# A two-layer graph network on one core: the second layer's first feed-forward product by block products, layer norm's rows on ScalarE, new durations in the plan

## The chip, the core and the metric

The kernel runs on one core of one Trainium2 chip. The metric is the device time of one execution in microseconds (us). The core has five engines, each with a queue of its own: TensorE (PE, matrix products; its weight loads appear as PEld), VectorE (DVE), ScalarE (ACT, which evaluates functions from loadable tables), GpSimd (POOL) and SyncE (SP, which here issues all the DMA transfers). Products land in PSUM, of which there are 8 banks of 512 float32 columns on 128 partitions. All is float32.

## The reference, cut to what matters

64 graphs of 256 nodes with 256 features go through two layers; each layer ends in a feed-forward block of width 1024 between two layer norms.

```python
# layer 0: two graph-attention steps, then
h = _layernorm(residual + h, g_ln1, b_ln1)
ff = jnp.matmul(jax.nn.relu(jnp.matmul(h, w_ff1) + b_ff1), w_ff2) + b_ff2
x = _layernorm(h + ff, g_ln2, b_ln2)
# layer 1: 8-head attention with a mask for each of 4 relations, then
x = _ln(src + attn_out, g1, beta1)
ff = jax.nn.gelu(x @ W1 + b1, approximate=False) @ W2 + b2
return _ln(x + ff, g2, beta2)
```

Layer norm is (x - mean) * rsqrt(var + 1e-5) * g + b over the 256 features of a node.

## The kernel before, in words

**Pairs and ways.** The 64 graphs are worked on as 32 pairs, so that a matrix product can have 512 columns (two graphs of 256 nodes). `whole_way` (L896) is a generator that takes one pair through everything: `gat_layers` (the two graph attentions), `feed_forward` with stage 0 (Relu), `attention` (stage 1), `feed_forward` with stage 2 (Gelu), then the output's DMA. Each `yield` stands before a step on TensorE and names the events it has to wait for, an exclusive name ("gat", "ff", "attention": one pair at a time) and the PSUM banks and buffers it takes.

**A plan decides the order.** `run` simulates the engines while the kernel is built. Three pairs are under way at once. At each moment it lets the engine go on that is free earliest; TensorE gets the first ready step, by preference one of the pair that holds "ff". Work for the other engines is handed in by `put(engine, us, emit, *events, ...)` with a duration, a rank, buffers it needs or frees, and a lag after which its result counts as there. The emitted order of each engine is then fixed (`keep_order`). On the chip each engine takes its instructions in this order and waits on real semaphores, so wrong durations in the plan change the order of work, not what is computed. Buffers are rings: `free` lists their slots for the plan, the `bufs` argument of `tile` makes them.

**First feed-forward product.** The input comes transposed as yT (features on partitions; two chunks of 128). Without blocks (stage 2 before, L651 to L660) each of 8 tiles of 128 hidden features is two accumulated products of 128x128 weights with 512 columns, and one activation of 512 columns out of PSUM. With blocks (stage 0, L565 to L653) the 2x2 block scheme of Winograd's variant of Strassen's method is used: two halves of the features, two halves of the 1024 hidden features, two halves of the nodes; seven block products in place of eight. `first_weights` loads the weights in four pieces into a tile of seven slots, `block_sums` forms three of the missing slots and one more by four VectorE operations at the start (L834). For each pair `sum_of_blocks` (L557) makes four 128x256 differences on VectorE, partly in place in yT, in the tile `sums_yT` (one buffer). `Slabs` stands for two of the four tiles of a half: its steps p1 to p7 are two 256-wide products each (L586); `evacuate` (L592) copies intermediate sums from PSUM by ScalarE, `add` (L598) adds others by VectorE, `activate` (L573) applies the function to 256 columns. p6 waits for p1's evacuation, p7 for p6's, p4 for p7's. The two objects a and b go through the steps in turn, in the order of the list at L650. One record of a float32 product in the profile stands for half of it: each product shows two.

**Second product** (L671): 32 products of 256 columns, followed by `add_rows` (L451, VectorE) and layer norm.

**Layer norm** (L453 to L480) works on one graph of the pair, two row tiles of 128x256: `statistics` on VectorE (L463, L464); `root` on GpSimd adds epsilon and raises to the power -0.5 (L467, L468); meanwhile `centre` on VectorE forms (x - mean) * g (L472), and `scale` on VectorE multiplies by the root and adds b (L476). It runs four times per pair for each graph: after the graph attentions, after each feed-forward block and after attention.

**The transposition.** `transposed` (L487) turns 32x32 blocks on VectorE (L496), stores them in memory (L501, SP) and gathers them as yT by four transfers (L507, SP); yT has three buffers. For a few `hurried` pairs at the start and the end TensorE transposes instead (L527). Stage 0 and 2 hold yT until the first product is done; attention copies it to yTa at once (L707, ScalarE).

Of the kernel before, what the change touches and what calls it, by code (L numbers as in the profile page):

```python
# [10 lines left out]
F32 = mybir.dt.float32  # L11
# [16 lines left out]
SLACK = 0.5  # L28
BY_BLOCKS = (0,)
START = {"tensor": 12.0, "vector": 11.0, "scalar": 12.0, "gpsimd": 0.0, "sync": 40.0}  # L30
# [3 lines left out]
def two_layers(ctx: ExitStack, tc: tile.TileContext, t: dict, out: bass.AP, flag: bass.AP):  # L34
# [91 lines left out]
    def bank():  # L126
# [11 lines left out]
    alone = {}  # L138
    free = {name: [0.0] * n for name, n in (("bank", 8), ("a", 2 * HQ), ("m", 2 * HQ), ("h", 2 * HQ), ("yb", 2), ("yT", 3), ("yTa", 1),
                                             ("xT", 1), ("rows", 1), ("e", 2), ("adjT", 1), ("adj", 3), ("sums", 1), ("x", 4))}  # L140
# [13 lines left out]

    def put(engine, us, emit, *events, rank=1, lag=0.15, kb=0, function=None, needs=None, frees=(), event=None):

        piece = {"engine": engine, "us": us, "emit": emit, "rank": rank, "lag": lag, "kb": kb, "function": function,
                 "needs": needs, "frees": frees, "event": event or Event(), "ready": 0.0, "missing": 0}  # L160
        for e in events:
            if e.time is None:
                piece["missing"] += 1
                e.then.append(piece)
            else:
                piece["ready"] = max(piece["ready"], e.time)
        if not piece["missing"]:
            waiting[engine].append(piece)
        return piece["event"]
# [190 lines left out]
    def gat_weights(y, at, at_home, ratio, there, to, empty, b):  # L360
# [20 lines left out]

        there = put("vector", 0.9, lambda: weigh(0), *there, rank=0, needs="e")
        there = put("vector", 1.0, lambda: weigh(1), there, rank=0, frees=["rows"] * b)
        return of, put("scalar", 0.85, scale, there, rank=0)

    def gat_layers(pair, to, loads):
# [12 lines left out]
        def evacuated(to, k, wide, ps):  # L399
            return put("scalar", 0.33, lambda: nc.scalar.activation(to[:, k, :wide], ps[:, :wide], AF.Copy),  # L400
                       took(0.88), frees=["bank"])
# [46 lines left out]
    def add_rows(y, p, b, *events):  # L448

        rows = y[:, of_graph(b), :].rearrange("p k d -> p (k d)")  # L450
        return put("vector", 0.65, lambda: nc.vector.tensor_tensor(rows, p, rows, ALU.add), *events, frees=["bank"])  # L451

    def layernorm(r, gb, b, *events):  # L453
        g, beta, _ = gb
        st = mv = rstd = None
        rows = [r[:, 2 * b + j, :] for j in range(2)]

        def statistics():
            nonlocal st, mv, rstd
            st, mv = small.tile([P, 2, 6], F32, name="st"), small.tile([P, 2, 2], F32, name="mv")  # L460
            rstd = small.tile([P, 2], F32, name="rstd")
            for j in range(2):
                nc.vector.bn_stats(st[:, j, :], rows[j])  # L463
                nc.vector.bn_aggr(mv[:, j, :], st[:, j, :])  # L464

        def root():
            nc.gpsimd.tensor_scalar(rstd, mv[:, :, 1], EPS, None, ALU.add)  # L467
            nc.gpsimd.tensor_tensor(rstd, rstd, mhalf[:, :2], ALU.pow)  # L468

        def centre():  # L470
            for j in range(2):
                nc.vector.scalar_tensor_tensor(rows[j], rows[j], mv[:, j, 0:1], g, op0=ALU.subtract, op1=ALU.mult)  # L472

        def scale():
            for j in range(2):
                nc.vector.scalar_tensor_tensor(rows[j], rows[j], rstd[:, j:j + 1], beta, op0=ALU.mult, op1=ALU.add)  # L476

        there = put("vector", 1.18, statistics, *events)
        power = put("gpsimd", 1.3, root, there)
        return put("vector", 0.95, scale, power, put("vector", 0.95, centre, there))  # L480

# [4 lines left out]
    def transposed(y, ready, to, b, pair, stage):  # L486
# [16 lines left out]
        def gather():  # L503
            if b == 0:
                to["yT"] = work.tile([P, 2, 4, KC * 64], F32, name="yT", bufs=3)
            for q in range(4):
                nc.sync.dma_start(to["yT"][32 * q:32 * q + 32, b],  # L507
                                  home[:, 128 * q:128 * q + 128].rearrange("(a j) n -> j a n", a=4))

        there = put("vector", 0.65, turn, ready, needs="yb")  # L510
        there = put("sync", 0.4, store, there, lag=1.3, kb=256, frees=["yb"])
        to[b] = put("sync", 1.75, gather, there, *([to[0]] if b else []), lag=1.7, kb=64, needs=None if b else "yT")

    def transposed_on_tensor(y, to):

        for b in range(2):
            if b == 0:
                yield [to[b]], None, 1, "yT"
                to["yT"] = work.tile([P, 2, 4, KC * 64], F32, name="yT", bufs=3)
            else:  # L520
                yield [to[b]], None, 1
# [14 lines left out]
    def feed_forward(y, normal, w, func, relieved, gb, pair, stage):  # L536
# [24 lines left out]
        if by_blocks:  # L561
            summed = [put("vector", 0.42, lambda: sum_of_blocks(0), normal[0], normal[1], rank=0, needs="sums")]
            for n in range(1, 4):
                summed.append(put("vector", 0.42, lambda n=n: sum_of_blocks(n), summed[-1], rank=0))

# [10 lines left out]
        class Slabs:  # L576
# [13 lines left out]
            def evacuate(self, name, rows, at, event):  # L590
                def copy():
                    nc.scalar.activation(self.rows[rows][:, :, at], self.bank["x"], AF.Copy)  # L592
                self.there[name] = put("scalar", 0.62, copy, event, rank=-1)

            def add(self, name, rows, at, bank, *events, frees=()):
                def add():
                    to = self.rows[rows][:, :, at]
                    nc.vector.tensor_tensor(to, self.bank[bank], to, ALU.add)  # L598
                self.there[name] = put("vector", 0.68, add, *events, rank=-1, frees=frees)

            def activate(self, rows, right, event):
                for n in range(2):
                    m, at = self.t + n + rows * half, columns[right]
                    of = self.rows[rows][:, n, at]
                    evacuated[right][m] = activate(of, of, m, 0.36, event, rank=right - 1)

# [22 lines left out]
            def p4(self):  # L629
# [4 lines left out]
                for n in range(2):  # L634
                    m = self.t + n + half
                    evacuated[0][m] = activate(self.rows[1][:, n, columns[0]], self.bank["x"][:, n], m, 0.36, there,
                                               rank=-1, frees=["bank"] * n)
# [8 lines left out]
        if by_blocks:  # L646
            a, b = Slabs(0), Slabs(2)
            for step in (a.p1, b.p1, a.p2, a.p6, b.p6, a.p5, a.p7, b.p7, b.p5, b.p2, a.p4, b.p4, a.p3, b.p3):
                yield from step()
            f = [f[m] for m in (0, 1, 4, 5, 2, 3, 6, 7)]  # L650
        else:  # L651
            for m in range(NF):
# [5 lines left out]
                if m % 2 == 0:  # L658
                    slabs()
                evacuated[0][m] = evacuated[1][m] = activate(f[m], p1, m, 0.6, took(1.72), frees=["bank"])  # L660
        frees_at(clock["tensor"], ["yT"] + ["sums"] * by_blocks)
# [27 lines left out]
    def projected(to, c, yT, w, bias, scale):  # L689
        ps = bank()  # L690
        for d in range(KC):
            nc.tensor.matmul(ps, lhsT=w[:, d, c * P:(c + 1) * P], rhs=yT[:, :, d, :], start=d == 0, stop=d == KC - 1)  # L692
        return put("scalar", 0.6, lambda: nc.scalar.activation(
            to[:, c, :], ps, AF.Identity, bias=bias[:, c:c + 1], scale=scale), took(1.72), relieved[1], frees=["bank"])

    def attention(y, normal, pair, all_adj):
# [12 lines left out]

        there = put("scalar", 0.55, lambda: in_one_piece(0), normal[0], needs="yTa")  # L710
        yield [put("scalar", 0.55, lambda: in_one_piece(1), there, normal[1], frees=["yT"])], "attention", 1
        qT, kT = (work.tile([P, KC, 512], F32, name=n) for n in ("qT", "kT"))
# [5 lines left out]
        def scores(n):  # L718
# [19 lines left out]
            def halves(o):  # L738
                h[n][o] = work.tile([P, N], F32, name="h", bufs=2 * HQ)
                nc.vector.tensor_tensor(h[n][o], a[n][o][:, :N], a[n][o][:, N:], ALU.add)  # L740

            there = [put("scalar", 0.52, lambda o=o: weight(o), there, rank=0, function="exp", needs="a", frees=["bank"])
                     for o in range(HQ)]
            masked.append([put("vector", 0.61, lambda o=o: mask(o), there[o], rank=0, needs="m") for o in range(HQ)] +
                          [put("vector", 0.36, lambda o=o: halves(o), there[o], rank=0, needs="h") for o in range(HQ)])

        def products(n):
# [18 lines left out]
            there = put("vector", 1.68, lambda: nc.vector.reciprocal(s, po[:, N:]), there, rank=0)  # L766
            there = put("vector", 0.36, lambda: nc.vector.tensor_tensor(to, po[:, :N], s, ALU.mult), there, rank=0)
            put("vector", 0.45, check, there, frees=["bank"])
# [82 lines left out]
    ln.append(layernorm_weights("L1_gnn_g1", "L1_gnn_beta1", "L1_gnn_b2"))  # L851
    ff1 = (weights("L1_gnn_W1p"), column("L1_gnn_b1"), weights("L1_gnn_W2"))
    ln.append(layernorm_weights("L1_gnn_g2", "L1_gnn_beta2"))
# [33 lines left out]
    def reliefs():  # L887
# [6 lines left out]
        yield [landed["ff1"]], None, 1  # L894
        put("vector", 0.0, lambda: None, relieve(ff1[1], lambda c, m: ff1[0][:, c, m * P:(m + 1) * P], ln[2][2]), event=relieved[2])

# [457 lines left out]
```

## Time and profile before

| | |
|---|---|
| median of 3 runs | 3125.2 us (3124.86 to 3127.16) |
| the profiled execution, whole | 3130.63 us |
| its span, first to last instruction | 3128.9 us |
| mean granted TensorE clock | 0.994 |
| VectorE: mask L736, 512 of 128x512 | 350.8 us busy |
| VectorE: L472 and L476 together, 1024 of 128x256 | 438.2 us busy |
| VectorE: statistics L463 and L464 | 208.5 and 93.2 us busy |
| GpSimd: L467 and L468, 256 each | 75.3 and 196.3 us busy |
| TensorE: L657, 1024 records of 512 columns | 457.1 us busy |
| TensorE: L586, 1024 and 768 records of 256 columns | 243.5 and 187.0 us busy |

A row of the profile names line, engine, operation, the tile written and the tiles read, the shape and the count, then the total busy time and the mean of one in ns. The mean holds a latency that overlaps with the next instruction of the same engine, so that the distance from one start to the next in the timeline is shorter than the mean. In the tables by stages each engine's busy time stands beside its count of instructions.

### The profile page before, as it was taken

The page shows a single profiled execution, that of the slowest core. Times are in us where ns is not written, and L with a number is a line of the kernel's source. Part 1 is how long each engine was busy: PE and PEld are TensorE (multiplying, and loading weights), DVE is VectorE, ACT ScalarE, POOL GpSimd, SP SyncE. Part 2 cuts the span into 40 slices and gives each one's busy share as a digit, 9 for nine tenths or more (in the row PEclk, how much of TensorE's full clock was granted, in tenths as well). Part 3 has the DMA queues.
Part 4 walks back from the last instruction along what each step waited for, and adds up shares of the span by engine and source line. Part 5 has one row for each costly group of instructions (what it writes and reads, how often), then busy time and mean ns, then how long its engine had stood idle before and what let it go on. Part 6 is the DMA issues. An engine that isn't in the chain of part 4 may idle for free.

```text
span 3128.9 us, 47274 instructions
## 1 busy us (share of the span) xinstructions
PE 3098.1 (99%) x17598; PEld 2165.6 (69%) x17598; DVE 2310.9 (74%) x5593; ACT 1308.1 (42%) x2552; POOL 272.3 (9%) x518
## 2 busy tenths in 40 slices
PE   7999999999999999999999999999999999999998
PEld 6766775686577668756865776687568657766855
DVE  5787677777767777777777677767777876787664
ACT  3444444443444444444434444444444344444432
POOL 0000100010010001000100100010001001000100
PEclk8999999999999999999999999999999999999999
DMA  6112311330132123113211320231132113102200
GB/s 190 42 35 68 108 41 41 95 95 32 44 109 67 35 68 108 41 41 97 93 33 43 113 67 31 68 108 41 41 102 88 35 47 110 64 31 68 67 2 15
DMA packets 210173, 205.41 MB, mean 66 GB/s; under 512 B 22161, under 2 KB 169745, under 8 KB 209937
## 3 DMA queue, kind: packets, MB, share of 16 engines
q1 hardware_dynamic: 209936, 202.32, 20.7%
q8 instruction: 141, 2.31, 0.3%
q14 instruction: 96, 0.78, 0.1%
HBM read 137.51 MB, written 64.73 MB: 65 GB/s over the span
## 4 chain that ended last, share of the span: by engine, by line
PE 97%; DVE 1%; DMA 1%; issue 1%; ACT 0%; SPq 0%; POOL 0%; POOLq 0%; DVEq 0%
PE ps L671 28%; PE ps L657 14%; PE ps L586 12%; PE ps L692 7%; PE ps L754 7%; PE ps L684 7%; PE ps L725 4%; PE ps L425 4%; PE ps L776 4%; PE ps L438 4%; PE ps L409 3%; PE ps L757 2%; PE ps L866 0%; PE ps L527 0%; DMA w_L_gnn_w_ff1p<-in_L_gnn_w_ff1p 0%
## 5 line engine op out<-in xcount | busy, mean ns | idle before, releaser
L671 PE MATMUL ps<-w_L_gnn_W,ff 128*128 128x256 f32 x2048 | 459.4, 381 | 0.0
L671 PE MATMUL ps<-w_L_gnn_w_ff,ff 128*128 128x256 f32 x2048 | 457.4, 380 | 0.0
L657 PE MATMUL ps<-yT,w_L_gnn_W1p 128*128 128x512 f32 x1024 | 457.1, 594 | 0.0
L736 DVE TENSOR_TENSOR m<-a,adj 128x512 f32<-128x512 f32 x512 | 350.8, 685 | 140.7 <-ACT a L732 140.7
L671 PEld LDWEIGHTS ps<-w_L_gnn_W,ff 128*128 128x128 f32 x2048 | 386.5, 190 | 75.3 <-issue 23.3
L671 PEld LDWEIGHTS ps<-w_L_gnn_w_ff,ff 128*128 128x128 f32 x2048 | 387.1, 190 | 60.7 <-issue 9.1
L732 ACT ACTIVATE a<-ps 128x512 f32<-128x512 f32 x512 | 265.6, 602 | 284.4 <-issue 177.9
L657 PEld LDWEIGHTS ps<-yT,w_L_gnn_W1p 128*128 128x128 f32 x1024 | 192.7, 190 | 215.4 <-issue 201.5
L467 POOL TENSOR_SCALAR rstd<-mv 128x2 f32<-128x2 f32 x256 | 75.3, 294 | 2827.9 <-DVE mv L464 2702.6
L766 DVE RECIPROCAL s<-ps 128x256 f32<-128x256 f32 x128 | 224.5, 1754 | 113.6 <-PE ps L757 113.6
L451 DVE TENSOR_TENSOR x<-ps,x 128x512 f32<-128x512 f32 x256 | 173.4, 677 | 129.4 <-PE ps L671 118.2
L573 ACT ACTIVATE ff<-ps,c_L_gnn_b 128x512 f32<-128x512 f32 x256 | 170.0, 686 | 234.5 <-PE ps L657 233.8
L586 PE MATMUL ps<-yT,w_L_gnn_w_ff1p 128*128 128x256 f32 x1024 | 243.5, 379 | 0.0
L684 PE MATMUL ps<-wv,yTa 128*128 128x512 f32 x512 | 238.7, 599 | 0.0
L592 ACT ACTIVATE ff<-ps 128x512 f32<-128x512 f32 x192 | 114.3, 596 | 268.7 <-PE ps L586 268.3
L370 DVE SCALAR_TENSOR_TENSOR e<-rows,ratio 128x256 f32<-128x256 f32 x256 | 122.2, 477 | 135.4 <-DMA rows<-row 123.1
L586 PEld LDWEIGHTS ps<-yT,w_L_gnn_w_ff1p 128*128 128x128 f32 x1024 | 194.3, 190 | 30.7 <-issue 4.6
L740 DVE TENSOR_TENSOR h<-a 128x256 f32<-128x256 f32 x512 | 213.7, 417 | 0.0
L463 DVE BATCH_NORM_STATS2 st<-x 128x6 f32<-128x256 f32 x512 | 208.5, 407 | 3.2
L400 ACT ACTIVATE xw<-ps 128x260 f32<-128x260 f32 (+1 forms) x256 | 97.8, 387 | 245.3 <-PE ps L409 181.7
L468 POOL TENSOR_TENSOR rstd<-rstd,mhalf 128x2 f32<-128x2 f32 x256 | 196.3, 767 | 21.4
L586 PE MATMUL ps<-sums_yT,w_L_gnn_w_ff1p 128*128 128x256 f32 x768 | 187.0, 382 | 0.0
(111 smaller groups left out, 4264.1 us busy)
## 6 DMA issues: line engine op xcount, KB each, us to landing
home<-yb SPq DMA_DIRECT2D x182, 256.0 KB, 2.0
yT<-home SPq DMA_DIRECT2D x728, 64.0 KB, 2.0
rows<-row SPq DMA_DIRECT2D x60, 512.0 KB, 3.9
xT<-in_xT SPq DMA_DIRECT2D x32, 512.0 KB, 3.8
x<-in_x SPq DMA_DIRECT2D x32, 512.0 KB, 4.0
out<-x SPq DMA_DIRECT2D x32, 512.0 KB, 3.4
adjT<-in_adjT SPq DMA_DIRECT2D x31, 512.0 KB, 5.2
w_L_gnn_w_ff1p<-in_L_gnn_w_ff1p SPq DMA_DIRECT2D x4, 256.0 KB, 6.0
```

The costliest lines, as they stand in the source:

```text
L463: nc.vector.bn_stats(st[:, j, :], rows[j])
L468: nc.gpsimd.tensor_tensor(rstd, rstd, mhalf[:, :2], ALU.pow)
L586: nc.tensor.matmul(self.bank[to][:, n], lhsT=w1[:, of, (self.t + n) * P:(self.t + n + 1) * P], rhs=rhs(), start=first and n == 0, stop=Tru ...
L657: nc.tensor.matmul(p1, lhsT=w1[:, c, m * P:(m + 1) * P], rhs=rhs, start=c == 0, stop=c == KC - 1)
L671: nc.tensor.matmul(p2[:, j * D:(j + 1) * D], lhsT=f[m][:, (2 * j + b) * P:(2 * j + b + 1) * P], rhs=w2[:, m, :], start=m == 0, stop=m == N ...
L684: nc.tensor.matmul(ps, lhsT=yT[:, b, c, jc * P:(jc + 1) * P], rhs=wv[:, c].rearrange("p r m -> p (r m)"), start=c == 0, stop=c == KC - 1)
L692: nc.tensor.matmul(ps, lhsT=w[:, d, c * P:(c + 1) * P], rhs=yT[:, :, d, :], start=d == 0, stop=d == KC - 1)
L732: nc.scalar.activation(a[n][o], ps[o], AF.Exp)
L736: nc.vector.tensor_tensor(m[n][o], a[n][o], adj, ALU.mult)
L740: nc.vector.tensor_tensor(h[n][o], a[n][o][:, :N], a[n][o][:, N:], ALU.add)
L754: nc.tensor.matmul(po[o * DH:(o + 1) * DH, :N], lhsT=v[b][:, jc, at:at + DH], rhs=e[o][:, jc * N:(jc + 1) * N], start=r == jc == 0, stop=r ...
L766: there = put("vector", 1.68, lambda: nc.vector.reciprocal(s, po[:, N:]), there, rank=0)
```

## The change

The second feed-forward block's first product takes the way by seven blocks too (`BY_BLOCKS`), with its weights in seven slots; yT goes from three buffers to two. Layer norm's rows are normalised by ScalarE, as root * x - mean * root, and VectorE multiplies by g and adds b in two operations over both row tiles, with g and b broadcast; epsilon is added on VectorE, and GpSimd multiplies -mean by the root. In the blocks b.p5 stands ahead of a.p7 now. Durations and the lag in the plan are set anew.

```diff
-BY_BLOCKS = (0,)
+BY_BLOCKS = (0, 2)
...
-    free = {... ("yT", 3), ...}
+    free = {... ("yT", 2), ...}
...
-    def put(engine, us, emit, *events, rank=1, lag=0.15, ...):
+    def put(engine, us, emit, *events, rank=1, lag=0.2, ...):
...
+            nc.vector.tensor_scalar(rstd, mv[:, :, 1], EPS, None, ALU.add)
+            nc.vector.tensor_scalar(less, mv[:, :, 0], -1.0, None, ALU.mult)

         def root():
-            nc.gpsimd.tensor_scalar(rstd, mv[:, :, 1], EPS, None, ALU.add)
             nc.gpsimd.tensor_tensor(rstd, rstd, mhalf[:, :2], ALU.pow)
-
-        def centre():
+            nc.gpsimd.tensor_tensor(less, less, rstd, ALU.mult)
+
+        def normalise():
             for j in range(2):
-                nc.vector.scalar_tensor_tensor(rows[j], rows[j], mv[:, j, 0:1], g, op0=ALU.subtract, op1=ALU.mult)
+                nc.scalar.activation(rows[j], rows[j], AF.Identity, bias=less[:, j:j + 1], scale=rstd[:, j:j + 1])

         def scale():
-            for j in range(2):
-                nc.vector.scalar_tensor_tensor(rows[j], rows[j], rstd[:, j:j + 1], beta, op0=ALU.mult, op1=ALU.add)
-
-        there = put("vector", 1.18, statistics, *events)
-        power = put("gpsimd", 1.3, root, there)
-        return put("vector", 0.95, scale, power, put("vector", 0.95, centre, there))
+            both = r[:, of_graph(b), :]
+            for v, op in ((g, ALU.mult), (beta, ALU.add)):
+                nc.vector.tensor_tensor(both, both, v.rearrange("p (k d) -> p k d", k=1).to_broadcast([P, 2, D]), op)
+
+        there = put("vector", 1.22, statistics, *events)
+        there = put("gpsimd", 1.2, root, there)
+        return put("vector", 1.2, scale, put("scalar", 0.8, normalise, there))
...
-            for step in (a.p1, b.p1, a.p2, a.p6, b.p6, a.p5, a.p7, b.p7, b.p5, b.p2, a.p4, b.p4, a.p3, b.p3):
+            for step in (a.p1, b.p1, a.p2, a.p6, b.p6, a.p5, b.p5, a.p7, b.p7, b.p2, a.p4, b.p4, a.p3, b.p3):
...
-    ff1 = (weights("L1_gnn_W1p"), column("L1_gnn_b1"), weights("L1_gnn_W2"))
+    ff1 = (first_weights("L1_gnn_W1p"), column("L1_gnn_b1"), weights("L1_gnn_W2"))
...
-        put("vector", 0.0, lambda: None, relieve(ff1[1], lambda c, m: ff1[0][:, c, m * P:(m + 1) * P], ln[2][2]), event=relieved[2])
+        relieve_first(ff1, ln[2][2], relieved[2])
```

In the plan alone, the durations change so (before, after, us): graph attention's weights on VectorE 0.9 and 1.0, 1.03 and 1.11; its scaling on ScalarE 0.85, 0.8; its evacuation 0.33, 0.4; `add_rows` 0.65, 0.6; the turn 0.65, 0.62; a block difference 0.42, 0.34; a block evacuation 0.62, 0.5; a block add 0.68, 0.6; an activation of 256 columns 0.36, 0.4, of 512 columns 0.6, 0.5; projections 0.6, 0.57; the copy to yTa 0.55, 0.52; attention's exps 0.52, 0.48; its halves and its division's product 0.36, 0.34.

## The prediction

> **What bounds the kernel now.** I read the engine shares first, then the stages, then single stretches in order of time. The page's first two parts:
>
> ```profile
> PE 3098.1 (99%) x17598; PEld 2165.6 (69%) x17598; DVE 2310.9 (74%) x5593; ACT 1308.1 (42%) x2552; POOL 272.3 (9%) x518
> PEclk8999999999999999999999999999999999999999
> ```
>
> The table by stages of the same trace (columns: stretch, its length, busy time of PE, PEld, DVE, ACT, POOL, granted clock, DMA share, GB/s):
>
> ```profile
> 0.00:30.00 30.00, 18.79 (x71) 15.75 (x72) 11.43 (x39) 7.90 (x18) 0.69 (x6) 0.81 0.84 250
> 30.00:60.00 30.00, 24.62 (x148) 20.48 (x147) 18.80 (x60) 11.14 (x32) 2.09 (x4) 0.84 0.63 194
> 973.00:1260.00 287.00, 287.00 (x1613) 200.50 (x1612) 216.92 (x525) 121.99 (x238) 26.16 (x50) 1.00 0.22 67
> 3000.00:3050.00 50.00, 46.23 (x412) 25.86 (x407) 37.06 (x79) 18.19 (x31) 3.25 (x6) 0.97 0.00 1
> 3100.00:3129.00 29.00, 19.05 (x78) 14.15 (x76) 6.95 (x20) 2.75 (x4) 2.32 (x4) 0.87 0.07 21
> ```
>
> The order of work repeats every three pairs (some 286.5 us), and in it TensorE is never idle, at full clock. Its 31 us of idle time lie at the start (11.2 + 5.4), at the end (3.8 + 10.0) and in 0.6 elsewhere. So for 2,900 us only TensorE's own work sets the time; the others matter only if they make it wait.
>
> The Trainium skill speaks against this reading: "Perfetto Trace Analysis" (Identifying the Most-Contended Engine) calls matmul busy time a bad measure and wants the share of weight loading, here 69%. By that there would be 31% of room and removing matmuls might win nothing. Spacing decides, not the busy column:
>
> ```profile
> 1183.69 13.90 PE L657 MATMUL ps<-yT,w_L_gnn_W1p 128*128 128x512 f32 x32
> 1197.42 2.75 PE L671 MATMUL ps<-w_L_gnn_W,ff 128*128 128x256 f32 x12
> ...
> 1221.68 2.75 PE L586 MATMUL ps<-yT,w_L_gnn_w_ff1p 128*128 128x256 f32 x12
> 1224.27 2.75 PE L586 MATMUL ps<-sums_yT,w_L_gnn_w_ff1p 128*128 128x256 f32 x12
> ...
> 1233.77 3.62 PE L671 MATMUL ps<-w_L_gnn_w_ff,ff 128*128 128x256 f32 x16
> ```
>
> Start to start, the second layer's 32 records (two to each of 16 products) take 13.73 us: 0.858 per 512-wide product. The first layer's 56 records, seven block products by four tiles, take 1233.77 - 1221.68 = 12.09: 0.432 per 256-wide product. Both run without a gap.
>
> **The main term.** The second layer's first product goes from 16 x 0.858 = 13.73 to 28 x 0.432 = 12.09 us a pair: 1.64 saved, for 32 pairs **-52.4 us**. (Not an eighth, 54.9: a narrow product costs slightly over half a wide one.)
>
> **What the blocks add elsewhere**, per pair, in spacings. VectorE: four differences at 0.34 (L740 to the next instruction) and six 512-wide adds at 0.61 (L736 to L740): 5.0. ScalarE: six evacuations at 0.49 (four of L732 in 2.06), sixteen Gelus at 0.40 (five 256-wide in 2.11) for eight at 0.575 (three in 1.84): 2.9 + 1.8 = 4.7. TensorE covers both; without cover the 9.7 us would be the pair's price.
>
> **Layer norm**, eight half-pairs per pair. Out: four L472/L476 instructions, two in 0.79 before the next: 1.58. In: two 512-wide VectorE operations, 1.21, and two tiny ones, 0.08 each by L375; so -0.2 on VectorE, -1.7 a pair. The broadcast operand isn't in the trace; L736's plain operands give 0.61, the slowest row per element (L370, two in 0.94) 0.94 for 512; I take 0.61, the same operation. ScalarE gets two Identity instructions; L380 (one per-partition scale) runs two in 0.90, spaced 0.80. With scale and bias both per partition there is no row; below, L380's 0.80, above, twice L573's largest 0.69: 1.4; I take 0.80: 6.4 a pair. GpSimd's second operation stays between L467's 0.29 and L468's 0.77, at 9% share.
>
> "ScalarE: Activation LUTs" (What ACT_TABLE_LOAD costs) in the Trainium skill adds about 93 ns for each per-partition operand. By it the two would cost about 1.0 (an estimate); no row here has both operands, and L380's duration holds one already.
>
> Sums: VectorE 72.2 + 5.0 - 1.7 = 75.5 of 93.9 us a pair (80%), ScalarE 40.9 + 4.7 + 6.4 = 52.0 (55%). VectorE's fullest stretches now, 1050:1070 (18.1 of 20) and 1130:1150 (18.6 of 20), cost TensorE nothing even there.
>
> **The table switch in the second layer's blocks.**
>
> ```profile
> L573 ACT ACT_TABLE_LOAD x63 | 80.8, 1283 | 1.1
> L732 ACT ACT_TABLE_LOAD x32 | 41.1, 1283 | 34.7 <-PE ps L725 34.3
> ```
>
> Two switches to Gelu a pair today. In the new order the first Gelu comes with p2's sum, its load holds the queue 1.28, and behind it wait the two Gelus and u2's evacuation, for which p7 waits. On the times of 1221.68: sum done 1225.2, load to 1226.6, Gelus to 1227.4, u2 out at 1228.1; p7 would be due at 1221.68 + 7 x 0.864 = 1227.7. So 0.35 us late, even with p5 of both halves moved ahead of p7 as cover. It shows only where no other pair has work: one pair in three (1183.69 is such a stretch). From 0 (all filled) to 32 x 0.35 = 11; I take 32/3 x 0.35 = **+3.7**.
>
> **The yT ring, three to two.** Following the gathers (L507) to their last readers through one period, never more than two are held: 1053.86 to 1108 beside 1065.45 to 1086.7, 1100.57 to 1163 beside 1161.73 to 1197, 1188.65 to 1233. **0**. The added stop would be on SP's queue: a late gather holds back nothing planned before it, and exposed it costs its chain, some 1.75 of issue + 2.0 landing for the second graph and 2.0 for the first, 5.7 us.
>
> **Start and end.** The four weight sums (L834, 0.69 each, 2.8 us) fall near 57 us, ahead of 6.61 us of VectorE idleness before L317 at 64.37: 0, up to 2.8. Three more DMA issues at some 0.4 each on SP lie before L1's weights are needed: 0. ScalarE's early normalising can hold up L380, for which TensorE already waits 1.11 at 57.33: 0 to 1.6, **+1**. After the last product the chain of the last layer norm grows by 0.16 (tiny operations), 0.95 (ScalarE, with its hand-over) and 0.42 (1.30 for 0.88 in the last step): **+1.5**. Twice before, pair 31's layer norms have little cover: the wait at 3027.69 (1.39, for yTa) takes the whole +1.5, the transposes at 3088.38 had 0.6 of slack: +0.9. The lags, durations and the order of p5 in the plan cost nothing by themselves; they move the order of emission, which the bounds below hold.
>
> **Sum:** -52.4 + 3.7 + 1.0 + 1.5 + 1.5 + 0.9 = **-43.8 us**. The span goes from 3128.9 to 3085. The profiled execution took 3130.63, 1.7 around its span and 5.4 over the median; on the median, 3125.2 - 43.8 = **3081**.
>
> **Rivals.** (1) Switching thrash: Gelus and the other pair's exps alternate (at 1075.81 to 1083 they already do, three loads in 7.3 us), so that u2 and u3 come out a further switch and back, 2.57, late in the two pairs of three where attention runs beside. Half hidden: 32 x (0.35 + 2/3 x 2.57 / 2) = 39, with the 4.9 of the ends: 3125.2 - 52.4 + 44 = 3117. For it: the blocks spread the Gelus over more steps; against it: just there attention gives TensorE work. (2) The narrow product is dearer than I think: by the page's busy times L586 costs 243.5 + 187.0 = 430.5 against 457.1, so only 26.6 is saved: 3125.2 - 26.6 + 8.6 = 3107. Against it: each group's busy time holds a modelled tail (2.75 for twelve that start 2.59 apart). (3) Slower: the two-deep yT ring. Longer norms shift the stages and a third gather comes due while two are held, ending as exposed idleness of 5.7 us. It decides from 43.8 / 32 / 5.7 = 0.24 such waits a pair; at one in three pairs 3081 + 32/3 x 5.7 = 3142, at one a pair 3264. For it: three slots exist now, and feed-forwards exclude one another; against: the holdings above.
>
> **Chances.** My forecast 0.74, with its own range 3066 to 3100: below, every addition at zero (3072.8), half of the 9.7 us of idleness outside the first and the last stretch reordered away, and some 2 of the slow clock at the start (0.81 to 0.84); above, all 11 of the table stall, 2.8, 1.6 and some 4 of new gaps. Thrash 0.12, dear products 0.03, ring 0.11. The range **3066 to 3110** leaves out about 0.2: the ring, most of the thrash, a little below. What a measurement can tell from no change is about 0.2%, 6 us. Faster 0.74 + 0.11 + 0.03 = 0.88; within, 0.01 of thrash and 0.02 of ring: 0.03; slower 0.09.
>
> **What would show it.** Right: TensorE still gapless over the middle with a period near 281.6 us for three pairs, 896 more products on the blocks' line and 512 fewer wide ones, VectorE near 80%, ScalarE near 55%. The stall would show as p7's line waiting for ScalarE's u2 by a few tenths; thrash as far over 125 table loads; the ring as TensorE waiting for the DMA yT. I am wrong if TensorE idles more than some 50 us in the middle.

## The result, and the profile after

The changed kernel takes 3093.45 us (median of 5 runs, 3091.06 to 3096.41) beside 3125.2 before: 31.75 us less, a ratio of 0.9896 (95% interval 0.9882 to 0.9911). The forecast was 3081, with a range of 3066 to 3110: the side and the range held, and 12 us of the 43.8 that were forecast are missing. The profiled execution took 3093.45 us, its span is 3091.7.

The engine shares and the granted clock of the changed kernel:

```profile
PE 3052.6 (99%) x18366; PEld 2309.3 (75%) x18366; DVE 2465.3 (80%) x5917; ACT 1622.4 (52%) x3452; POOL 265.9 (9%) x518
PEclk8999999999999999999999999999999999999999
```

VectorE stands at 80% and ScalarE at 52%, where 80 and 55 were forecast; TensorE still bounds the kernel. The stages, in the columns of the prediction's table:

```profile
0.00:30.00 30.00, 18.77 (x78) 15.56 (x79) 12.70 (x40) 8.45 (x20) 0.70 (x6) 0.89 0.79 248
30.00:60.00 30.00, 25.02 (x150) 20.81 (x149) 20.19 (x62) 13.11 (x37) 1.79 (x4) 0.83 0.65 195
973.00:1260.00 287.00, 286.74 (x1705) 215.57 (x1704) 232.33 (x556) 153.31 (x327) 24.83 (x48) 1.00 0.21 68
3000.00:3050.00 50.00, 43.63 (x360) 31.75 (x363) 36.45 (x84) 23.69 (x42) 4.29 (x8) 0.99 0.00 1
3062.00:3091.00 29.00, 18.63 (x88) 16.05 (x86) 10.26 (x25) 8.59 (x20) 1.77 (x4) 0.87 0.07 21
```

The middle holds 0.26 us of idle TensorE in 287, where it held none. The stretch 3000:3050 holds 6.4 in 50, but it lies nearer to the end than it did; over the last 170 us TensorE is idle for 20.3, where it was idle for 13.6. The rows of groups that the change touches:

```profile
L474 ACT ACTIVATE x<-x,less,rstd 128x256 f32<-128x256 f32 x512 | 279.1, 593 | 416.0 <-POOL less L470 414.6
L479 DVE TENSOR_TENSOR x<-x,b_L_gnn_beta 128x512 f32<-128x512 f32 x128 | 88.5, 692 | 4.4
L470 POOL TENSOR_TENSOR less<-less,rstd 128x2 f32<-128x2 f32 x256 | 59.0, 230 | 20.1
L576 ACT ACT_TABLE_LOAD x33 | 42.3, 1283 | 0.4
L735 ACT ACT_TABLE_LOAD x12 | 15.4, 1283 | 21.8 <-PE ps L728 21.8
```

The broadcast operand costs VectorE hardly more than a plain one: 670 to 692 ns in its four groups, for the mask's 683. An Identity with scale and bias both per partition takes 593 ns, 89 more than the 504 of L380 with one. That agrees with the 93 ns per operand of "ScalarE: Activation LUTs" (What ACT_TABLE_LOAD costs) in the Trainium skill, and two of them run 1.09 where L380's two run 0.91. All table loads together fell from 126 to 66; far over 125 would have been the sign of the first rival's thrash.

**A ledger.** To see where the 12 us went, I took the distance from the start of each TensorE record to the start of the next. The usual distance of each kind of record, summed, is the matrix work; what a distance has over the usual one is loss, booked to the place where it lies. The rows add up to the span (us):

| kernel | matrix work | loss to 100 us | middle | last 170 us | after the last product |
|---|---|---|---|---|---|
| before (run again) | 3046.7 | 25.7 | 29.9 | 12.8 | 9.8 |
| after | 2994.4 | 25.9 | 38.2 | 22.0 | 11.2 |
| difference | -52.3 | +0.3 | +8.3 | +9.2 | +1.4 |
| forecast | -52.4 | +1.0 | +3.7 | +2.4 | +1.5 |

The matrix term came true to 0.1 us. What is missing lies in the middle and in the last 170 us. (The 29.9 that was there before lies mostly at the switches between small and large tiles, as many in both kernels, and isn't idleness.) Three pairs now take 282.35 us on average over 24 pairs, for 286.42 before and 281.6 forecast.

**The middle.** The timeline of the changed kernel where the chain that the prediction worked out comes true (start, duration, engine, line):

```profile
1061.24 3.62 PE L589 MATMUL ps<-sums_yT,w_L_gnn_W1p 128*128 128x256 f32 x16
...
1062.30 1.28 ACT L576 ACT_TABLE_LOAD   x1
...
1063.59 0.91 ACT L576 ACTIVATE ff<-ff,c_L_gnn_b 128x256 f32<-128x256 f32 x2
...
1064.41 1.06 ACT L595 ACTIVATE ff<-ps 128x512 f32<-128x512 f32 x2
...
1065.03 1.13 PE L589 MATMUL ps<-yT,w_L_gnn_W1p 128*128 128x256 f32 x4 [0.17 <-ACT ff L595]
1066.09 1.07 PE L757 MATMUL ps<-a,v 128*32 128x256 f32 x16
```

This is p7 behind u2 (the first of the two at L595), behind two Gelus, behind the load. Sixteen records should take 16 x 0.216 = 3.46 us; the next group starts 3.79 after the first of them: 0.33 late, where 0.35 was forecast. Then its own first record is 0.10 longer than usual (0.32 for 0.216).

The place isn't the forecast one. The prediction expected the wait in the one pair of three beside which no attention runs. Here another pair's attention runs beside (L757 comes next), only not between these blocks; in the pair without attention, small products of the graph attention (L438 at 1163.67 and 1166.26) come between the blocks, and p7 at 1170.57 does not wait.

A second wait, which I had not seen, comes once per period where VectorE's adds (L601) stand in a row of three behind the graph attention's weights (L372, at 891.40):

```profile
891.81 1.88 DVE L601 TENSOR_TENSOR ff<-ps,ff 128x512 f32<-128x512 f32 x3
...
892.73 2.14 PE L589 MATMUL ps<-yT,w_L_gnn_W1p 128*128 128x256 f32 x8
...
893.74 0.73 PEld L589 LDWEIGHTS ps<-yT,w_L_gnn_W1p 128*128 128x128 f32 x4 [0.38 <-DVE ff L601]
```

The eight records are p3 of both halves; the last four start 0.14 late, at 893.74, and the first of these is 0.10 longer again. Both waits come once in three pairs; the middle holds 10.0 periods, so they make 4.3 and 2.4 of its 8.3.

**The last 170 us** of the changed kernel, TensorE's timeline, with what ended each gap:

```profile
3016.34 1.13 PE L589 MATMUL ps<-yT,w_L_gnn_W1p 128*128 128x256 f32 x4 [2.01 <-ACT a L735]
...
3029.06 1.99 PE L674 MATMUL ps<-w_L_gnn_W,ff 128*128 128x256 f32 x8 [1.68 <-ACT ff L576]
...
3046.35 1.08 PE L530 MATMUL ps<-ident,x 128*32 128x128 f32 x32 [0.29 <-DVE x L479]
3049.82 1.94 PE L530 MATMUL ps<-ident,x 128*32 128x128 f32 x32 [2.39 <-DVE x L479]
3052.47 3.78 PE L589 MATMUL ps<-yT,w_L_gnn_W1p 128*128 128x256 f32 x8 [0.71 <-ACT yT L534]
```

The first gap names exps of the last pair's attention: on ScalarE the load of their table (3014.39) and four of them run first. The second is the second product waiting for its last Gelus, which stand behind four more exps with a load before and after them (3023.82 to 3028.48). That is the first rival's switching, in the last pairs. The third, fourth and fifth are the last layer norm and its transposition, with nothing else to run. The 32 transposes at 3049.82 take 1.94 for the 1.08 of the same 32 at 3046.35: in 3049.50:3052.00 the granted clock is 0.50. It stays there until 3056.3, so the first block records from 3052.47 on come 0.427 apart, too, for 0.216.

### The profile page after: what moved, and what is told of

Its sections match the earlier page's. It is cut to its first block, busy times and chain, and to the rows that moved or that the text cites. A ratio compares the mean times of both kernels' runs of the same rounds, so it can differ in the third digit from the quotient of the medians.

```text
span 3091.7 us, 50645 instructions
## 1 busy us (share of the span) xinstructions
PE 3052.6 (99%) x18366; PEld 2309.3 (75%) x18366; DVE 2465.3 (80%) x5917; ACT 1622.4 (52%) x3452; POOL 265.9 (9%) x518
## 3 DMA queue, kind: packets, MB, share of 16 engines
q1 hardware_dynamic: 210240, 202.32, 20.3%
## 5 line engine op out<-in xcount | busy, mean ns | idle before, releaser
L474 ACT ACTIVATE x<-x,less,rstd 128x256 f32<-128x256 f32 x512 | 279.1, 593 | 416.0 <-POOL less L470 414.6
L735 ACT ACTIVATE a<-ps 128x512 f32<-128x512 f32 x512 | 272.3, 603 | 395.2 <-PE ps L728 395.1
L674 PE MATMUL ps<-w_L_gnn_w_ff,ff 128*128 128x256 f32 x2048 | 462.6, 381 | 0.0
L674 PE MATMUL ps<-w_L_gnn_W,ff 128*128 128x256 f32 x2048 | 458.7, 380 | 1.7 <-ACT ff L576 1.7
L469 POOL TENSOR_TENSOR rstd<-rstd,mhalf 128x2 f32<-128x2 f32 x256 | 206.2, 806 | 2797.2 <-DVE less L466 2598.4
L674 PEld LDWEIGHTS ps<-w_L_gnn_w_ff,ff 128*128 128x128 f32 x2048 | 386.5, 190 | 70.8 <-issue 20.7
L674 PEld LDWEIGHTS ps<-w_L_gnn_W,ff 128*128 128x128 f32 x2048 | 388.2, 190 | 66.4 <-issue 12.9
L595 ACT ACTIVATE ff<-ps 128x512 f32<-128x512 f32 x384 | 223.4, 590 | 220.9 <-PE ps L589 220.2
L601 DVE TENSOR_TENSOR ff<-ps,ff 128x512 f32<-128x512 f32 x384 | 249.0, 681 | 26.4 <-PE ps L589 19.7
L589 PE MATMUL ps<-yT,w_L_gnn_W1p 128*128 128x256 f32 x1024 | 248.3, 386 | 4.5 <-ACT a L735 2.0
L687 PEld LDWEIGHTS ps<-wv,yTa 128*128 128x128 f32 x512 | 94.7, 190 | 120.3 <-issue 120.1
L589 PE MATMUL ps<-sums_yT,w_L_gnn_w_ff1p 128*128 128x256 f32 x768 | 180.6, 381 | 0.4 <-DVE sums_yT L560 0.4
```

The source lines that it names most:

```text
L474: nc.scalar.activation(rows[j], rows[j], AF.Identity, bias=less[:, j:j + 1], scale=rstd[:, j:j + 1])
L589: nc.tensor.matmul(self.bank[to][:, n], lhsT=w1[:, of, (self.t + n) * P:(self.t + n + 1) * P], rhs=rhs(), start=first and n == 0, stop=Tru ...
L674: nc.tensor.matmul(p2[:, j * D:(j + 1) * D], lhsT=f[m][:, (2 * j + b) * P:(2 * j + b + 1) * P], rhs=w2[:, m, :], start=m == 0, stop=m == N ...
L687: nc.tensor.matmul(ps, lhsT=yT[:, b, c, jc * P:(jc + 1) * P], rhs=wv[:, c].rearrange("p r m -> p (r m)"), start=c == 0, stop=c == KC - 1)
L735: nc.scalar.activation(a[n][o], ps[o], AF.Exp)
```

## The experiments

Times are medians; each kernel ran beside the kernel before on the same chip, whose medians were 3126.91 (the runs named e1 to e4), 3126.24 (e5 to e8) and 3127.28 (e9 to e12).

**e1_before_again: the kernel before, unchanged.** One execution, for a second profile of before.

> The kernel before, unchanged, profiled a second time. The first profiled execution lay 5.4 us over the median. If that was the start (granted clock 0.81 and 0.84 in the first 60 us, first block product at 69.34), this one has the first block product near 66 to 67 and a span near 3124 to 3126, with the same 286.4 us for three pairs. If it was spread over the whole span, the period differs.

3126.56 us, span 3124.8: 4.1 under the first profile. Of that, 3.4 lies ahead of the first block product (65.94 us for 69.34), as in the changed kernel (66.18): the first profile had a granted clock of 0.81 in its first 30 us, for 0.89. It was the start, then, and the ledger goes by this profile.

**e4_blocks_old_norm: the change without the layer norm's move.** The function `layernorm` is that of the kernel before.

> The changed kernel with layer norm as before (two steps on VectorE, with their old durations in the plan). Theory (blocks bring it all, the longer norm costs some 4 to 7 us at the end): period 281.5 to 282.6, the last stretch shorter, time 3086 to 3091. Rival (VectorE, at some 82% then, makes TensorE wait, and the move of the norm to ScalarE was needed): time over 3096, TensorE waiting for VectorE's masks or sums.

3090.91 us, ratio 0.9883 (0.9867 to 0.9900): as good as the whole change or a little better; the intervals overlap. The theory holds. Middle 37.9 for 38.2, last 170 us 20.0 for 22.0, end 9.5 for 11.2. The norm's move brings nothing here, and the 1.7 us at the end is its price there.

**e9_blocks_alone: e4 with all the old durations and the old lag too.**

```diff
-    def put(engine, us, emit, *events, rank=1, lag=0.2, ...):
+    def put(engine, us, emit, *events, rank=1, lag=0.15, ...):
...
-                self.there[name] = put("scalar", 0.5, copy, event, rank=-1)
+                self.there[name] = put("scalar", 0.62, copy, event, rank=-1)
...
-                    evacuated[right][m] = activate(of, of, m, 0.4, event, rank=right - 1)
+                    evacuated[right][m] = activate(of, of, m, 0.36, event, rank=right - 1)
```

> The blocks in the second layer, the new step order and the two-deep ring, with the old layer norm and all the old durations and the old lag in the plan: what the main part of the change brings alone. Theory A (the plan's durations and lag are needed wherever the new blocks are, because with the old ones the plan's time is shorter than the chip's and the order drifts): near the 3217 us of the kernel with all the old durations, 3190 to 3225, with the waits for Gelu outputs before the second product again. Theory B (it was the mixture of the new norm's steps with old durations that upset the order): like the kernel with the old norm and the new durations, 3091, at most 3100.

3098.05 us, ratio 0.9908 (0.9892 to 0.9925). Theory B holds: the blocks alone, in the old plan, already bring 29 of the 32 us. The loss in the middle is 46.0 for e4's 37.9.

**e3_norm_wide: the norm's move, the durations, the ring and the place of p5 without the second layer's blocks** (`BY_BLOCKS = (0,)`, the second layer's weights loaded as before).

> The changed kernel with the second layer's first product wide again; norm on ScalarE, two yT buffers and the new durations stay. Theory (norm, ring and durations cost the middle nothing, only the ends): three pairs take 286.4 us as before and the time is 3126 to 3131. Rival (the longer norm chain stalls the middle too): period over 287 and time over 3135. Rival (the new durations alone win some of the time): under 3122.

3138.12 us, ratio 1.0034 (1.0022 to 1.0047): slower by 11, and 9.2 of it in the middle (39.1 for 29.9), only 2.1 at the end, none in the last 170 us. The theory, which put the cost at the ends, falls; the first rival's figures fit (three pairs take 287.44). Blocks of the first layer now wait for ScalarE, five times for exps (L735), 3.6 us.

**e6_before_new_durations: the kernel before with the new durations and lag, nothing else.**

> The kernel before with the new durations and lag in its plan and nothing else. The kernel with the wide product, the new norm and the new durations lost 11 us against the kernel before, 9 of it in the middle. Theory A (the durations do it): 3131 to 3137 here too, TensorE waiting inside the first layer's blocks. Theory B (the norm on ScalarE does it, its work standing in ScalarE's queue before the blocks' evacuations): 3124 to 3129.

3131.09 us, ratio 1.0016 (1.0007 to 1.0026): +5, of it 3.3 in the middle and 1.8 in the last 170 us. The time falls on the lower edge of theory A's range, and blocks of the first layer wait for VectorE's adds, four times, 2.4 us. Of e3's 9.2 in the middle about 3 thus came with the durations' order; the rest came with the norm, the shorter ring or the place of p5, which no run here tells apart.

**e5_old_durations: the whole change with the old durations and lag** (those of e9; the norm's own stay new, since its steps are new).

> The changed kernel with the durations and the lag of the plan as they were before (the new layer norm keeps its own). The changed kernel loses some 8 us more than the kernel before inside its middle, in waits of a few tenths. Theory A (the plan's new, shorter durations place steps of the blocks a few tenths too early): the middle's waits go, 3083 to 3088. Theory B (the Gelu's table load and the block's queue on ScalarE and VectorE make them, whatever the durations): 3090 to 3097, with waits of a few tenths at p7 and p3 still.

3217.0 us, ratio 1.0294 (1.0277 to 1.0311). Both theories fall: it is 124 us slower than the changed kernel, with the same instructions, but for 90 more table loads, in another order. The waits of TensorE (total, times, longest):

```profile
PE ps L674 <- ACT ff L576: 37.8, 18, 2.9
PE ps L589 <- ACT xw L380: 24.7, 6, 4.3
PE ps L589 <- DMA yT<-home: 12.6, 3, 4.7
```

ScalarE in one of nine such places, and the second product that waits for it:

```profile
1161.12 0.83 ACT L576 ACTIVATE ff<-ps,c_L_gnn_b 128x256 f32<-128x256 f32 x2
1161.96 1.28 ACT L735 ACT_TABLE_LOAD   x1
1163.26 0.60 ACT L735 ACTIVATE a<-ps 128x512 f32<-128x512 f32 x1
1163.87 1.28 ACT L576 ACT_TABLE_LOAD   x1
1165.17 3.31 ACT L576 ACTIVATE ff<-ff,c_L_gnn_b 128x256 f32<-128x256 f32 x8
...
1167.33 1.35 PE L674 MATMUL ps<-w_L_gnn_W,ff 128*128 128x256 f32 x5 [2.89 <-ACT ff L576]
```

One exp between the Gelus costs a load there and a load back, and the second product is 2.89 late. This is akin to my first rival, the switching thrash, near the size that I gave it (2.57, without the exp itself), though what waits is the second product and not p7: it exists, and it comes or not with the order that the plan draws. The loads are 156 here, 66 in the changed kernel. The loss in the middle is 160.0; the nine waits of 2.89 are 26 us of it, and the waits for L380 and for yT stand beside them.

**e10_block_durations: the changed kernel with the feed-forward's old durations alone** (difference 0.42, evacuation 0.62, add 0.68, activations 0.36 and 0.6).

> The changed kernel with only the feed-forward's own durations set back in the plan (block difference 0.42, evacuation 0.62, add 0.68, activations 0.36 and 0.6); lag 0.2 and everything else new. Theory A (what upset the order with all the old durations was that the plan counted 0.36 for a Gelu of 256 columns that takes 0.40, so that it put the second product ahead of its Gelus): over half of the 124 us comes back, 3155 or more, as waits of the second product's line L674 for ScalarE. Theory B (it was the lag of 0.15 for the hand-over between engines, or the sum of all): at most 20 us, 3090 to 3115.

3124.55 us, ratio 0.9992 (0.9983 to 1.0002): 31 us, so the gain is gone. It lies between the theories, and the mechanism of A is not there: no wait of L674 for Gelus is among the large ones (though the table loads are 128), but many others are, at other places:

```profile
PE ps L530 <- DVE x L479: 11.7, 3, 6.2
PE ps L589 <- ACT xw L380: 9.4, 5, 2.8
...
PE ps L589 <- ACT a L735: 6.5, 9, 0.7
PE ps L589 <- DVE s L766: 5.8, 8, 0.9
```

**e2_no_load: Relu for Gelu, in the same order on every engine.** It leaves out the Gelu, and with it every load of its table.

```diff
-            return put("scalar", us, lambda: nc.scalar.activation(to, p, func, bias=b1[:, m:m + 1]), *events, relieved,
+            return put("scalar", us, lambda: nc.scalar.activation(to, p, AF.Relu, bias=b1[:, m:m + 1]), *events, relieved,
```

> The changed kernel with Relu evaluated in place of Gelu in the second feed-forward block, so that no table is switched; the plan still counts the switch, and the order of every engine stays. Leaves out the Gelu. Theory (u2's evacuation stands behind the table load and p7 waits for it): the waits of p7 vanish, three pairs take 281.5 in place of 282.5 us, the time falls by 8 to 13 us to some 3083. Rival (ScalarE is late from its new norm and evacuation work): period and time stay within 2 us of the changed kernel's 282.5 and 3093.5.

3085.16 us, 8.3 less than the changed kernel. The size is as expected, the place only in part: in the middle 4.2 (34.0 for 38.2), in the last 170 us 2.7; the wait at 3029.06 is gone with the load, and p3's wait for VectorE stays. (The profiled execution is the slowest of four; its span is 5.9 shorter.) So the load costs 4.2 in the middle, near the 4.3 of the timeline, and the other 4.1 of the middle's 8.3 has other causes, p3's wait the largest. Three pairs take 282.02 us, not the 281.5 of the theory: 0.33 a period is regular, and the rest of the 4.2 is not.

**e7_p2_late: p2, whose sum starts the first Gelu, after p7 in the second layer.**

```diff
-            for step in (a.p1, b.p1, a.p2, a.p6, b.p6, a.p5, b.p5, a.p7, b.p7, b.p2, a.p4, b.p4, a.p3, b.p3):
+            late = (a.p1, b.p1, a.p6, b.p6, a.p5, b.p5, a.p7, b.p7, a.p2, b.p2, a.p4, b.p4, a.p3, b.p3)
+            early = (a.p1, b.p1, a.p2, a.p6, b.p6, a.p5, b.p5, a.p7, b.p7, b.p2, a.p4, b.p4, a.p3, b.p3)
+            for step in late if stage == 2 else early:
```

> The changed kernel with p2 of both halves moved behind p7 in the second layer's blocks, so that the first Gelu, and with it the table load, comes after u2's and u3's evacuations. Theory (the load in front of u2 makes p7 wait, 0.34 and 0.10 for starting again, in one pair of three): that wait goes, 0.44 x 10.7 = 4.7 us less, some 3088 to 3090, and no wait of p7 for ScalarE longer than 0.1. Rival (the load only moves to another place, where the second product waits for its first Gelus): no gain, 3092 to 3098, the second product's line waiting for ScalarE.

3109.33 us, ratio 0.9946 (0.9929 to 0.9962): 16 slower than the changed kernel. The load was put elsewhere, and the order changed with it. p7's waits behind the load are gone, as the theory said, but waits of the blocks for exps (7.3 us in ten) and for the graph attention's small blocks (L345, 5.1 in nine) took their place. The rival was right that nothing is gained, but its range ended at 3098, and the second product does not wait.

**e12_table_price: the plan counts 1.9 instead of 1.3 us for a switch of the table.**

```diff
-                clock[engine] += 1.3
+                clock[engine] += 1.9
```

> The changed kernel with 1.9 instead of 1.3 us counted in the plan for a switch of ScalarE's table. Theory A (the plan places p7 too early because it prices the switch without what stands around it; priced higher, it gives other work to TensorE there): the middle's loss falls from 38 to about 34, 3088 to 3091. Theory B (a fixed order drawn from a plan with one wrong price is no better than another: the gain at one place is lost at others): 3093 to 3110.

3095.59 us, ratio 0.9902 (0.9885 to 0.9918). Theory B: the middle loses more, 49.1, with L438 waiting for ScalarE's L380 eleven times (11.5 us for 3.9). But the last 170 us lose only 15.0, with the same work and the norm still on ScalarE: the 22.0 of the changed kernel is not fixed by its work.

**e8_short_last: the last pair's norms after attention and after both feed-forwards on VectorE, as before.**

```diff
+    def layernorm(r, gb, b, *events, short=False):
+        if short:
+            return layernorm_short(r, gb, b, *events)
...
+                                  short=pair == NPAIR - 1)
```

> The changed kernel with the last pair's layer norms after attention and both feed-forward blocks done as before (two steps on VectorE). The last 170 us lose 22.0 us on TensorE for 12.8 before, and 1.4 more come after the last product. Theory (the longer norm chain does it where nothing covers it): 1.5 at the very end and 3 to 5 at the transposes of the last pair are won back, 3087 to 3090. Rival (the blocks' own waits with little other work do it): only the 1.5 at the end, 3091 to 3093.

3087.86 us, ratio 0.9879 (0.9862 to 0.9895), 5.6 less than the changed kernel and the fastest here that computes the reference; the theory's range holds. The last 170 us lose 18.5 for 22.0, the end takes 9.3 for 11.2, and the middle stands at 37.9. TensorE's timeline at the two waits for the last pair's norm:

```profile
3046.82 1.26 PE L561 MATMUL ps<-ident,x 128*32 128x128 f32 x32 [0.17 <-DVE x L510]
3048.79 2.86 PE L620 MATMUL ps<-yT,w_L_gnn_W1p 128*128 128x256 f32 x12 [0.72 <-ACT yT L565]
```

The wait of 2.39 and the half clock behind it are gone. Another half clock came: 0.50 in 3016.85:3020.25, behind the wait of 2.01 for exps that the changed kernel has, too, at full clock. The intervals against the changed kernel's overlap; the two profiles' spans differ by 7.5.

**e11_short_wide_last: e8, and the last pair's second layer without blocks.** For that pair one quarter of the weights is replaced by a stored sum of two quarters, so its values differ; the amount of work is that of the wide product.

> The changed kernel with the last pair's late norms on VectorE as before and, for the last pair alone, the second layer's first product without blocks. Theory (what is left of the tail's loss, 18.5 us against 12.8 before, is the blocks' chain with no other pair to cover it): the loss in the last 170 us falls by 3 to 5 for 1.64 us of added matrix work, so 3084 to 3087 beside the 3088 of the kernel with the short norms alone. Rival (the loss is fixed by the order that the plan finds at the end, whichever form it has): no fall, 3088 to 3092.

3090.15 us, ratio 0.9881 (0.9865 to 0.9898): no gain, and the last 170 us lose 20.7 for e8's 18.5. The rival was right: the remaining loss isn't the blocks' chain of that one pair.

## Why the prediction was right, and where it was not

**The main term was right**, -52.3 for -52.4: the new blocks' records come as densely as those of the first layer's blocks, and all that they make TensorE wait for stands in the other columns. Reading it from spacing was what made it right: by busy times the second layer's blocks cost 248.3 + 177.8 = 426.1 for 457.1, 31.0 less, and the second rival rested on that column. The share of weight loading, 69% before and 75% now, foretold neither.

**The load ahead of p7 was right** in mechanism and size: 0.33 us for 0.35 at one place, 4.2 for 3.7 in sum by e2. That it comes once in three pairs was luck: the pair is not the one that the prediction named, for the reason shown above.

**The end was right**, 1.4 for 1.5. At the start 0.3 came for 1.0; **the ring** cost nothing: TensorE never waits for yT's gathers in the changed kernel, and with two slots in the kernel before the plan draws the same order on all five engines. In other orders such waits come: 12.6 us in three (e5, 4.7 at the longest), 3.9 in three (e9), 3.6 in two (e10). So the third rival's wait exists; whether a third slot would spare it wasn't tried.

**What failed is the sentence "The lags, durations and the order of p5 in the plan cost nothing by themselves".** I counted the order's effect as a bound of a few us, and as nothing in the sum. By e6 the new durations alone cost the kernel before 5 us. With the blocks the order is the largest lever after the matrix work: of the kernels with 2994.4 of matrix work and the Gelu, the middle loses 37.9 (e4, e8), 38.2 (after), 46.0 (e9), 49.1 (e12), 51.5 (e7), 64.4 (e10) and 160.0 (e5). In the changed kernel itself the part that I left out is small, p3 behind VectorE's three adds and 1.6 us that I can't name; in the others it is mostly waits that repeat in each period, from tenths of a us to 4.7, each kernel's at places of its own. For the same reason e2 alone gives the price of one cause in the middle: it keeps the order, while the other edits can draw a new one as well.

**Mis-sized is the term for the last pairs**, "Twice before, pair 31's layer norms have little cover", +1.5 and +0.9: 9.2 came. With the last pair's norms moved back (e8) 3.5 of it goes, more than the 2.4 forecast for the norm: the wait at 3049.82 takes 2.39, and the clock fell behind it. Without the Gelu's table loads (e2) 2.7 goes: the term left out the switching between Gelus and exps in the last pairs. But neither is a fixed price: e3, with the norm moved and no blocks, loses no more there than before, and e12, with norm, Gelus and blocks, only 2.2 more. So the term counted the length of one chain and not the order of the work around it; how the 9.2 divides stays open.

The terms that failed are thus short by 4.6 (middle) and 6.8 (last pairs), less 0.7 at the start; with 1.4 between the difference of the two profiles (33.1) and that of the medians they make the 12.

**That layer norm's move is part of a gain was never shown.** e4 does without it and is no slower; e3, which has it without the blocks, is slower. I had put its price on the engines under cover: VectorE's 1.7 us a pair were no gain, since VectorE, at 74 to 80% of the span, bounds nothing.

## What to carry to other kernels

Where one engine is gapless, count the spacing of its instructions and the matrix work of a change can be forecast to a tenth of a us; what surrounds it cannot be had so closely. Where a plan made while building fixes the order, a changed duration is a change of the kernel: the same work took 3093 or 3217 us, so try several settings of the plan for each change, and book the loss by stage before praising one. Relieving an engine that ends no wait is worth nothing, and its new partner can end one.

## What the runs showed of the hardware

A gap of TensorE costs more than its length. After a gap at full clock the first 256-column record is some 0.10 us longer (0.29 to 0.32 for 0.216 from start to start; after, e5, e8, e12). After longer ones the clock can fall to half: in e5, none of nine gaps of 1.31 us was followed by spacings of 0.427, five of nine gaps of 2.89 were, and all nine of 3.4 to 4.7, for 1.0 to 6.1 us, half of which is lost. So the same gap of 2.89 cost 3.0 us or up to 4.8. The gap of 2.01 for exps was followed by it in e8 and not in the changed kernel.

"TensorE: Matmul & The Clock Gate" (What's actually happening) in the Trainium skill has the clock follow a free-running window of 3.4 us, which agrees with the part that chance plays; but its table asks for a whole idle window, and here 2.89 us were enough five times in e5, and 2.39 at 3049.82 and 2.01 in e8 behind small products.
